# Loading the last nine rounds' input in mid-run, in three loads of three rounds, in a kernel that writes all pairwise products

## Chip, cores, metric

One core of a Trainium2 chip. The metric is device time in microseconds (us), the median of several executions. Every run told of here was at a granted clock of 1.0.

## The reference

```python
# inputs: (4096, 256) float32
d = inputs.shape[1]
dot = jnp.einsum('bi,bj->bij', inputs, inputs)
iu, ju = jnp.triu_indices(d)
return dot[:, iu, ju]          # (4096, 32896) float32
```

4.2 MB come in and 539 MB go out; there is one multiplication per output.

## The kernel before

The input is a tile `xt` of 128 partitions with 32 rows each. A round is two rows per partition, so there are 16 rounds. The output columns of a round are cut into five chunks; VectorE (DVE) and ScalarE (ACT) share the products of a chunk, and two stores send it out. Three output buffers rotate. The very first chunk is stored in four pieces, so that the stores begin early.

```python
opool = ctx.enter_context(tc.tile_pool(name="o", bufs=3))
...
cuts = [0, REPEAT * d, total // 2, total]        # rounds 0, 1-7, 8-15
for a, b in zip(cuts, cuts[1:]):
    nc.sync.dma_start(xt[:, a:b], x_in[:, a:b])

for g in range(groups):                          # 16 rounds
    for c, (lo, hi) in enumerate(zip(borders, borders[1:])):   # 5 chunks
        o = opool.tile([P, REPEAT, slot], F32, tag="o", ...)
        first = g == c == 0
        cuts = [lo, *(FIRST if first else []), hi]
        for a, b in zip(cuts, cuts[1:]):
            ...                                  # products on ACT and DVE
            for r in range(REPEAT):
                nc.sync.dma_start(x_out[g][:, r, a:b], o[:, r, a - lo : b - lo])
```

Loads and stores all go through SyncE's queue.

Of the kernel before, what the change touches and what calls it, by code (L numbers as in the profile page):

```python
# [1 line left out]

# [4 lines left out]

F32 = mybir.dt.float32
AF = mybir.ActivationFunctionType
ALU = mybir.AluOpType  # L10

P = 128
UNIT = 64
REPEAT = 2
PIECES = 5
BUDGET = 0.95
FIRST = [512, 1536, 3584]


def even_borders(lo: int, hi: int, pieces: int) -> list[int]:  # L20
    units = (hi - lo) // UNIT
    return [lo + units * c // pieces * UNIT for c in range(pieces)] + [hi]


def runs(d: int, lo: int, hi: int) -> list:


    found, at = [], 0
    for i in range(d):
        a, b = max(at, lo), min(at + d - i, hi)  # L30
        if a < b:
            found.append((i, i + a - at, a, b - a))
        at += d - i
    return found


def vector_ops(block: list) -> list:




    ops, k = [], 0
    while k < len(block):
        i, j, at, n = block[k]
        m = 2 if k + 2 < len(block) and i == j else 1
        ops.append((block[k], m))
        k += m
    return ops


def interleave(block: list) -> list:


    half = len(block)
    while half and len(vector_ops(block[:half])) > len(vector_ops(block[half:])):
        half -= 1
    a, b = vector_ops(block[:half]), vector_ops(block[half:])
    return [op for k in range(max(len(a), len(b))) for ops in (a, b) for op in ops[k : k + 1]]


def vector_time(block: list) -> float:
    return sum(68 + 1.046 * REPEAT * n * m for (*_, n), m in vector_ops(block))


def split(block: list, budget: float) -> int:


    scalar, k = 0.0, 0
    while k < len(block):
        scalar += REPEAT * (184 + 0.837 * block[k][3])  # L70
        if vector_time(block[k:]) <= budget or scalar > vector_time(block[k + 1 :]):
            break
        k += 1
    return k


def window(ap: bass.AP, free: list) -> bass.AP:
    return bass.AP(ap.tensor, ap.offset, [list(ap.ap[0]), *free])


@with_exitstack
def kernel(
    ctx: ExitStack, tc: tile.TileContext, x: bass.AP, out: bass.AP
):





    nc = tc.nc  # L90
    n, d = x.shape
    width = out.shape[1]
    assert n % (P * REPEAT) == 0 and width == d * (d + 1) // 2 and width % UNIT == 0
    groups = n // (P * REPEAT)
    borders = even_borders(0, width, PIECES)
    slot = max(b - a for a, b in zip(borders, borders[1:]))

    xpool = ctx.enter_context(tc.tile_pool(name="x", bufs=1))
    opool = ctx.enter_context(tc.tile_pool(name="o", bufs=3))

    x_in = x.rearrange("(p r) d -> p (r d)", p=P)
    x_out = out.rearrange("(p g r) c -> g p r c", p=P, r=REPEAT)


    total = n // P * d
    xt = xpool.tile([P, total + 1], F32, name="x")
    nc.vector.memset(xt[:, total:], 0.0)  # L107
    cuts = [0, REPEAT * d, total // 2, total]
    for a, b in zip(cuts, cuts[1:]):
        nc.sync.dma_start(xt[:, a:b], x_in[:, a:b])  # L110

    for g in range(groups):
        for c, (lo, hi) in enumerate(zip(borders, borders[1:])):
            o = opool.tile([P, REPEAT, slot], F32, tag="o", name=f"o_{g}_{c}")
# [3 lines that stand above are left out]
                block = runs(d, a, b)  # L118
                k = split(block, 0.0 if first else BUDGET * REPEAT * (b - a))
                for i, j, at, length in block[:k]:  # L120
                    for r in range(REPEAT):
                        row = (g * REPEAT + r) * d
                        nc.scalar.activation(  # L123
                            o[:, r, at - lo : at - lo + length],
                            xt[:, row + j : row + j + length],
                            AF.Copy,
                            scale=xt[:, row + i : row + i + 1],
                        )
                row = g * REPEAT * d
                for (i, j, at, length), m in interleave(block[k:]):  # L130
                    at -= lo
                    nc.vector.tensor_tensor(  # L132
                        o[:, :, at : at + m * length],
                        window(xt[:, row + j :], [[d, REPEAT], [1, m], [1, length]]),
                        window(xt[:, row + i :], [[d, REPEAT], [1, m], [0, length]]),
                        ALU.mult,
                    )
                for r in range(REPEAT):
                    nc.sync.dma_start(x_out[g][:, r, a:b], o[:, r, a - lo : b - lo])  # L139


# [1 line left out]
_INS = ["r_inputs"]  # L143
_OUTS = [((4096, 32896), "float32")]


# [20 lines left out]
```

## Time and profile before

| | before |
|---|---|
| time, median (range) of 3 runs | 1274.32 us (1274.27 to 1274.36) |
| bytes through the store and load queue | 543.17 MB |
| share of the span in which the transfer engines work for it | 99.8% |
| VectorE / ScalarE busy | 78% / 38% |

The kernel is a queue with compute in front of it. One therefore looks first at when the queue is idle or slow, and at compute only where the queue waits for it. The prediction below shows the lines. One view it doesn't show is needed later: the stretches of the kernel before around the time when chunk 1 is issued (26.69 us). In the stretches the columns are start and end, length, busy time of the engines with the number of instructions, clock, share of the transfer engines, GB/s.

### The profile page before, as it was taken

The numbers are of one execution on the slowest core, as the hardware profiler recorded it, in microseconds if no ns is written. First come the engines' busy times: TensorE is split into PE (matmuls) and PEld (weight loads), VectorE is DVE, ScalarE is ACT, GpSimd is POOL, SyncE is SP. The second block draws the span as 40 slices with busy tenths as digits, with TensorE's granted clock in tenths as the row PEclk, the third lists the DMA queues.
The fourth block names the chain that finished last, engine by engine and source line by source line (L and its number), as shares of the span: only waits on it lengthen the run. The fifth ranks groups of instructions, "written<-read, shape, count | busy, mean of one in ns | idle before, by whom it ended". The sixth has DMA issues, their size and how long they took to land.

```text
span 1272.5 us, 3975 instructions
## 1 busy us (share of the span) xinstructions
DVE 996.1 (78%) x1813; ACT 486.7 (38%) x1547; POOL 0.2 (0%) x4
## 2 busy tenths in 40 slices
DVE  8987887878777787777877777777777777777770
ACT  5523535234342433424334252342523425234250
POOL 0000000000000000000000000000000000000000
DMA  9999999999999999999999999999999999999998
GB/s 384 435 433 430 434 433 427 434 432 427 431 428 432 429 430 431 429 431 429 433 427 431 429 431 429 431 430 430 429 432 427 433 427 432 428 432 429 431 427 346
DMA packets 24367, 543.43 MB, mean 427 GB/s; under 512 B 2704, under 2 KB 2704, under 8 KB 3344
## 3 DMA queue, kind: packets, MB, share of 16 engines
q1 hardware_dynamic: 24336, 543.17, 99.8%
q14 instruction: 31, 0.25, 0.0%
HBM read 4.19 MB, written 538.97 MB: 427 GB/s over the span
## 4 chain that ended last, share of the span: by engine, by line
DMA 70%; DVE 25%; issue 1%; SPq 1%; DVEq 0%
DMA out_dram<-o 70%; DVE o L132 25%; SPq L139 1%; DMA x<-in_r_inputs_dram 1%; DVEq L132 0%; SPq L110 0%
## 5 line engine op out<-in xcount | busy, mean ns | idle before, releaser
L132 DVE TENSOR_TENSOR o<-x 128x356 f32<-128x356 f32 (+61 forms) x1812 | 996.1, 634 | 239.9 <-DMA out_dram<-o 191.1
L123 ACT ACTIVATE o<-x 128x253 f32<-128x253 f32 (+41 forms) x1546 | 485.4, 404 | 748.6 <-DMA out_dram<-o 732.8
L123 ACT ACT_TABLE_LOAD x1 | 1.3, 1283 | 0.7 <-PEq L154 0.7
L107 DVE MEMSET x<- 128x1 f32 x1 | 0.1, 59 | 0.8 <-PEq L154 0.8
L154 POOL MEMSET const-uint8-127<- 128x1 uint8 x1 | 0.1, 102 | 0.0
L154 POOL MEMSET const-bfloat16-1.0<- 128x1 bf16 x1 | 0.1, 101 | 0.0
L154 POOL MEMSET const-float32-0.0<- 128x1 f32 x1 | 0.1, 98 | 0.2 <-issue 0.2
L154 POOL MEMSET const-float32-1.0<- 128x1 f32 x1 | 0.1, 98 | 0.0
## 6 DMA issues: line engine op xcount, KB each, us to landing
out_dram<-o SPq DMA_DIRECT2D x128, 3296.0 KB, 27.2
out_dram<-o SPq DMA_DIRECT2D x30, 3264.0 KB, 28.9
out_dram<-o SPq DMA_DIRECT2D x2, 1472.0 KB, 13.3
x<-in_r_inputs_dram SPq DMA_DIRECT2D x1, 2048.0 KB, 12.3
out_dram<-o SPq DMA_DIRECT2D x2, 1024.0 KB, 10.0
x<-in_r_inputs_dram SPq DMA_DIRECT2D x1, 1792.0 KB, 6.8
out_dram<-o SPq DMA_DIRECT2D x2, 512.0 KB, 10.2
out_dram<-o SPq DMA_DIRECT2D x2, 256.0 KB, 10.0
```

The costliest lines, as they stand in the source:

```text
L107: nc.vector.memset(xt[:, total:], 0.0)
L123: nc.scalar.activation(o[:, r, at - lo : at - lo + length], xt[:, row + j : row + j + length], AF.Copy, scale=xt[:, row + i : row + i + 1],)
L132: nc.vector.tensor_tensor(o[:, :, at : at + m * length], window(xt[:, row + j :], [[d, REPEAT], [1, m], [1, length]]), window(xt[:, row + ...
L139: nc.sync.dma_start(x_out[g][:, r, a:b], o[:, r, a - lo : b - lo])
L154: nc = _bacc.Bacc("TRN2", target_bir_lowering=False, num_devices=1)
```

## The change

Its intent: only the input of the first seven rounds is fetched before the stores begin; the rest follows in mid-run, so that the first stores don't wait behind input that is not needed for hundreds of microseconds.

```diff
+AHEAD = 7
+LOADED = 3
...
-    cuts = [0, REPEAT * d, total // 2, total]
-    for a, b in zip(cuts, cuts[1:]):
+    def load(g: int, end: int):
+        a, b = g * REPEAT * d, end * REPEAT * d
         nc.sync.dma_start(xt[:, a:b], x_in[:, a:b])
+    load(0, 1)
+    load(1, AHEAD)
...
                 for r in range(REPEAT):
                     nc.sync.dma_start(x_out[g][:, r, a:b], o[:, r, a - lo : b - lo])
+            if c == 0 and g and g % LOADED == 0 and g - LOADED + AHEAD < groups:
+                load(g - LOADED + AHEAD, min(g + AHEAD, groups))
```

## The prediction

> **What bounds the kernel now.** I read the page's summary first, for busy shares, slices and queues.
>
> ```profile
> span 1272.5 us, 3975 instructions
> DVE 996.1 (78%) x1813; ACT 486.7 (38%) x1547; POOL 0.2 (0%) x4
> ...
> DMA  9999999999999999999999999999999999999998
> GB/s 384 435 433 430 434 433 427 434 432 427 431 428 432 429 430 431 429 431 429 433 427 431 429 431 429 431 430 430 429 432 427 433 427 432 428 432 429 431 427 346
> ...
> q1 hardware_dynamic: 24336, 543.17, 99.8%
> ...
> HBM read 4.19 MB, written 538.97 MB: 427 GB/s over the span
> ```
>
> The one queue keeps 16 transfer engines busy for 99.8% of the span; VectorE (DVE) is busy for 78% and ScalarE (ACT) for 38%. The kernel is bound by bytes: 543.17 MB at about 430 GB/s. The change moves no byte away, so in mid-run there is nothing to gain. Only the first slice (384 GB/s) and the last (346) fall short. The end is the same in both kernels, so the question is the start. The waits show the steady state: both engines wait for buffers that a store has to free, that is, for the queue.
>
> ```profile
> ACT o L123 <- DMA out_dram<-o: 732.8, 75, 12.5
> DVE o L132 <- DMA out_dram<-o: 191.1, 59, 4.0
> ```
>
> Next the timeline of the first 60 us (start, length) and, of the transfer issues of the loads, the time to landing.
>
> ```profile
> 0.73 1.34 SPq L110 DMA_DIRECT2D x<-in_r_inputs_dram  x3
> ...
> 3.41 4.28 DVE L132 TENSOR_TENSOR o<-x 128x512 f32<-128x512 f32 x9 [2.55 <-DMA x<-in_r_inputs_dram]
> ...
> 8.02 52.23 DVE L132 TENSOR_TENSOR o<-x 128x988 f32<-128x988 f32 x90 [0.33 <-DMA x<-in_r_inputs_dram]
> ```
>
> ```profile
> x<-in_r_inputs_dram SPq DMA_DIRECT2D x1, 2048.0 KB, 12.3
> ...
> x<-in_r_inputs_dram SPq DMA_DIRECT2D x1, 1792.0 KB, 6.8
> ```
>
> Two things to see. VectorE starts at 3.41, when only the first load (round 0) is in; the second lands near 8 us and the third near 13 us. And from 8.02 on it runs without a gap. So the ramp up is set by compute, unless the queue is behind it. Which of the two it is, the stretches with the transfer share and GB/s (last two columns) and the store issues tell.
>
> ```profile
> 1.50:2.00 0.50, 0.00 (x0) 0.50 (x1) 0.00 (x0) 1.00 0.35 49
> 2.00:7.00 5.00, 3.59 (x8) 3.60 (x11) 0.00 (x0) 1.00 1.04 406
> ...
> 0.00:26.69 26.69, 23.01 (x33) 17.07 (x45) 0.20 (x4) 1.00 0.94 374
> ...
> 30.00:1260.00 1230.00, 969.79 (x1777) 469.63 (x1502) 0.00 (x0) 1.00 1.00 430
> ```
>
> ```profile
> 26.69 0.84 SPq L139 DMA_DIRECT2D out_dram<-o  x2
> ```
>
> I call a fifth of the output columns of one round (two rows per partition) a chunk; the first chunk is stored in four pieces of 512, 1024, 2048 and 2944 columns. Their stores are issued at 4.80, 6.74, 11.21 and 14.40 us (same timeline, in short windows); those of chunk 1 at 26.69 us. By then the queue has moved 26.69 us x 374 GB/s = 9.98 MB, out of the loads (4.19 MB) and chunk 0 (128 partitions x 2 rows x 6528 columns x 4 B = 6.68 MB), together 10.87 MB. So it is 0.89 MB, or 2.1 us, behind when chunk 1 arrives, and gets to it at about 28.8 us. That 2.1 us is all that fewer bytes at the start can win.
>
> **What the Trainium skill says.** "DMA: Bandwidth & Descriptors", section Queues, rings and completion order: descriptors on one ring are consumed in ring order. The trace agrees: the first store, issued at 4.80, takes some 10 us to land behind the loads. So a load in mid-run takes its turn in the same line as the stores and displaces them by its own length. The same page, section Where 436 GB/s comes from, puts the ceiling of the fabric at 435 GB/s; the steady 430 here is within 1.2% of it, which leaves no idle room in which a load could hide. The same page, section Latency and other measured facts, gives a memory access as 0.2 us on average and 2 us at high load; the trace of before has no load beside stores in mid-run, so it doesn't show this, and I keep it as a risk.
>
> **The change part by part.**
> Removed from the start: the first loads now bring rounds 0 to 6 and not 0 to 15. That is 9 rounds x 512 floats x 4 B x 128 partitions = 2.36 MB less, 5.5 us at 430 GB/s. The remaining 1.84 MB are in when the queue has moved as much, at about 6.5 us (49 GB/s for 0.5 us, then 406).
>
> What the queue does with the time: piece 1 (0.52 MB, issued 4.80) goes from 6.5 to 7.8; piece 2 (1.05 MB, issued 6.74) to 10.3. Piece 3 is issued at about 11 us, since VectorE makes it by then. From an issue to the first bytes are some 1.2 us here (first load: issued 0.73, bytes just before 2.0). So it runs from 12.2 to 17.1, and piece 4 (3.0 MB, issued 14.40) to 24.1. Then the queue is empty until chunk 1. VectorE saves its wait of 0.33 us at 8.02 (the load that it waits for is 0.26 MB, 0.6 us, shorter), so chunk 1 is issued at 26.4 and its bytes start at 27.6. Before they start at 28.8. **Gain at the start: 1.2 us**, and not 5.5: the rest turns into idle time of the queue, near 11 and from 24 to 27.6 us.
>
> After that the queue doesn't run dry again: a chunk takes 6592 x 1024 B = 6.75 MB, 15.7 us, to store and about 12.4 us to compute; chunk 2 was issued at 39.0, while chunk 1 goes on until 43.3.
>
> Added in mid-run: three loads of 0.786 MB, each 1.83 us of the full queue. All of it is on the path that sets the end, since the queue is always backed up. **Cost: 5.5 us.**
>
> Added inefficiency: loads are not quite at full rate. In before the second load moved some 2 MB at 406, an excess of 0.3 us; the third had 2.1 MB from 7 to 13 us, 6.0 us in place of 4.9, an excess of about 1 us. I take 0.3 us for each of the smaller new loads, towards the low end. **Cost: 0.9 us.**
>
> Issues and waits: three issues of 0.42 us on SyncE, hidden behind a backlog of more than a store. The buffers come free 1.8 us later after each load, but the product of the delay is again the queue's time, already counted. Nothing is computed anew.
>
> Sum: 1274.3 - 1.2 + 5.5 + 0.9 = **1279.5 us**, 0.4% slower.
>
> **The rivals.**
> (a) Dependence by whole tile: the mid-run load writes the tile of the input that every operation reads. If the order is kept for the whole tile, the operations after each load wait until it lands. A store takes 27.2 us from issue to landing in steady state; the load behind it would land 2 us later, with an empty queue, which then waits some 12.4 us of compute and 2 to 3 us of latencies. Three times 15 is 45 us: about 1320 us. Against it: in before VectorE started at 3.41 while two loads into the same tile were under way; only the operation at 8.02 waited, one of those on a pair of rows, whose window reaches one element into the next round. So the order is kept by region, and of rounds 0 to 6 only round 6 reaches into round 7's region, long after its load. I give this 3%.
> (b) The queue never empties at the start, or loads and stores overlap, so that the mid-run loads cost nothing: time 1273 us, at best. For it: the third load's slow stretch (1 us) leaves the start. Against it: chunk 1's issue time is VectorE's, which runs without a gap, and in the trace loads occupy the engines at no higher rate than stores do. I give 8%.
> (c) Loads among stores are slow, a packet taking twice as long while the memory is loaded with writes: each costs another 1.8 us, or 1284 to 1286 us. For it: the slow third load. Against: that slow stretch had no stores beside it at all, so the cause is another. I give 12%.
>
> **Range and chances.** The middle case, 77%, spans the excess of the loads from 0 to 1 us each and the uncertainty of 1 us at the start: 1277.5 to 1281.5. I widen it towards (c) and somewhat towards (b): 1276.5 to 1283.0. Two per cent are 25 us: only (a) reaches that. Faster by over 2% would need 25 us less transfer, and the bytes are the same: 0.5%. Slower by over 2%: 3.5%. Within 2%: 96%.
>
> **What would show it right or wrong.** In the profile after: the first slice's rate falls from 384 to about 325 GB/s (1.84 + 6.68 MB, and 1.8 MB of chunk 1 from 27.6 on, over 31.8 us); the first two loads land 0.6 us earlier; VectorE's wait of 0.33 us at 8 us is gone; chunk 1 is issued at 26.4; the transfer share of the whole falls to some 99.4%; the slices with a mid-run load still show 430 GB/s, with 0.79 MB of it being input; the waits of VectorE for the input stay under 4 us. The prediction is wrong if VectorE waits for a load in mid-run (a), if the slices with loads show clearly more than 435 GB/s (b), or if they fall by more than some 10 GB/s each (c). It is also wrong if chunk 1's issue comes earlier than 26 us.

## More of the kernel before

```profile
24.00:25.00 1.00, 1.00 (x2) 0.00 (x0) 0.00 (x0) 1.00 0.99 424
25.00:26.00 1.00, 1.00 (x2) 0.00 (x0) 0.00 (x0) 1.00 1.03 436
26.00:27.00 1.00, 1.00 (x3) 0.00 (x0) 0.00 (x0) 1.00 0.99 424
```

The queue is full: it still works on chunk 0.

## The result, and the profile after

| | before | after |
|---|---|---|
| time, median | 1274.30 us (4 runs, one more than above) | 1279.12 us (1278.81 to 1279.59, 4 runs) |
| span of the profiled run | 1272.5 us | 1277.3 us |
| ratio | | 1.0038 (95%: 1.0021 to 1.0055) |

A ratio is the mean time of one kernel's runs over that of the other's in the same rounds, so not quite the ratio of the medians. It is 4.8 us slower by the medians, and also by the two profiled spans.

The page of the kernel after, the lines that answer to those of before:

```profile
span 1277.3 us, 3976 instructions
...
GB/s 358 435 429 428 435 423 434 431 426 435 427 431 432 425 435 410 430 434 431 432 433 431 422 424 432 432 434 433 431 430 432 430 427 435 424 434 430 427 434 322
...
q1 hardware_dynamic: 24624, 543.17, 99.5%
```

The first slice fell from 384 to 358. In mid-run one slice stands out with 410, the 16th (479 to 511 us), and a pair of 422 and 424 (the 23rd and 24th). A page like this dates the loads. There are two such places, and not three. The prediction had named a fall of more than some 10 GB/s in such a slice as a sign of rival (c), slow loads among stores; the 410 is such a fall.

The timeline of SyncE, first 60 us of the kernel after, tells where the third one is:

```profile
4.79 2.77 SPq L145 DMA_DIRECT2D out_dram<-o  x4
7.60 0.79 SPq L113 DMA_DIRECT2D x<-in_r_inputs_dram  x1
10.78 41.73 SPq L145 DMA_DIRECT2D out_dram<-o  x10
```

A load at 7.60 us: the program's scheduler moved the first of the three forward, from round 3 to the space between the stores of the second and the third piece, where SyncE had nothing to do. The built program's order shows it too (a listing of SyncE's instructions, not a profile):

```
L145 DMACopy out_dram<-o_0_65 128x1024 [waits Activation_49]
L113 DMACopy x<-in_r_inputs_dram 128x1536
L145 DMACopy out_dram<-o_0_65 128x2048 [waits DVE_49,Activation_49]
```

It waits for nothing, since no operation had read its target. The diff alone doesn't show this. The two other loads were issued where the source puts them:

```profile
467.39 1.25 SPq L113 DMA_DIRECT2D x<-in_r_inputs_dram  x1
...
705.95 1.26 SPq L113 DMA_DIRECT2D x<-in_r_inputs_dram  x1
```

The stretches of the kernel after, at the start:

```profile
11.00:12.00 1.00, 1.00 (x2) 1.00 (x4) 0.00 (x0) 1.00 0.47 156
12.00:13.00 1.00, 1.00 (x2) 1.00 (x4) 0.00 (x0) 1.00 0.85 285
...
25.00:26.00 1.00, 1.00 (x3) 0.00 (x0) 0.00 (x0) 1.00 0.56 236
26.00:27.00 1.00, 1.00 (x3) 0.00 (x0) 0.00 (x0) 1.00 0.06 24
27.00:28.00 1.00, 1.00 (x3) 0.56 (x2) 0.00 (x0) 1.00 1.00 422
```

and the issue of chunk 1's stores, from the timeline of SyncE:

```profile
26.25 0.81 SPq L145 DMA_DIRECT2D out_dram<-o  x2
```

The early load lies where the queue would have been short of work (11 to 13 us), and the queue still runs dry before chunk 1, which VectorE has ready at 26.25 us. Chunk 1's bytes flow from about 27.1 us; in before the queue came to them at about 28.8. The packet records agree: chunk 1's first packet starts at 27.08 us, and in before at 28.81. (The packed trace holds start, length and size of every packet; no view of the profile prints them one by one.) So the start gained 1.7 us. The span grew by 4.8 us, so from there on 6.5 us were lost, for two loads whose bytes alone take 2 x 1.83 = 3.7. What the rest is, the stretches around the second load show (it was issued at 467 us and is carried out when the stores ahead of it are):

```profile
492.00:494.00 2.00, 2.00 (x3) 0.00 (x0) 0.00 (x0) 1.00 0.97 418
...
496.00:497.00 1.00, 0.73 (x3) 0.00 (x0) 0.00 (x0) 1.00 1.71 418
497.00:498.00 1.00, 0.00 (x0) 0.00 (x0) 0.00 (x0) 1.00 0.29 89
498.00:499.00 1.00, 0.00 (x0) 0.00 (x0) 0.00 (x0) 1.00 1.03 253
499.00:500.00 1.00, 0.00 (x0) 0.00 (x0) 0.00 (x0) 1.00 0.89 303
500.00:501.00 1.00, 0.00 (x0) 0.00 (x0) 0.00 (x0) 1.00 1.26 525
```

These are not all equally exact: a packet seems to be booked whole to one stretch, so a 1 us stretch can read over 1 or over the steady rate. The sum is safer: 418, 89, 253, 303 and 525 are 1588 over 5 us, 318 GB/s on average, where the steady rate is 430. That is 5 x (1 - 318/430) = 1.3 us lost around this one load. Its packet records put part of that on the load's own packets and part on the last stores before it, which took 1.6 to 2.0 us instead of 0.98.

No operation waited for a load in mid-run. The waits of the kernel after:

```profile
DVE o L138 <- DMA out_dram<-o: 205.5, 62, 5.7
...
DVE o L138 <- DMA x<-in_r_inputs_dram: 2.5, 1, 2.5
```

The one wait for the input is that at the very start; the 0.33 us at 8 us are gone.

### The profile page after: what moved, and what is told of

Its sections match the earlier page's. It is cut to its first block, busy times and chain, and to the rows that moved or that the text cites. A ratio compares the mean times of both kernels' runs of the same rounds, so it can differ in the third digit from the quotient of the medians.

```text
span 1277.3 us, 3976 instructions
## 1 busy us (share of the span) xinstructions
DVE 995.6 (78%) x1813; ACT 486.6 (38%) x1547; POOL 0.2 (0%) x4
## 3 DMA queue, kind: packets, MB, share of 16 engines
q1 hardware_dynamic: 24624, 543.17, 99.5%
## 4 chain that ended last, share of the span: by engine, by line
DMA 70%; DVE 25%; SPq 1%; issue 1%; DVEq 0%
DMA out_dram<-o 70%; DVE o L138 25%; SPq L145 1%; DMA x<-in_r_inputs_dram 0%; DVEq L138 0%
```

## The experiments

My theory after the result: a load in mid-run costs its bytes and 1.4 us on top, for the change of direction in the queue; the early load was nearly free because it lay in an idle gap. The 1.4 is (6.5 - 3.7) / 2. The rivals: the excess goes with the bytes; any small transfer among large ones pays it; or it is not the loads in mid-run at all.

Each time stands beside about 1274.2 to 1274.3 us for the kernel before on the same chip.

### One: let all three loads be in mid-run (the first attempt missed)

Rounds 7 to 9 go to the places of rounds 0 to 2, so that their load can't be issued before round 2 is used up. (Here and in number nine the cut leaves out a renamed variable, the same index in the lines that compute, and one or two memsets of one column, which moved the first store from 4.79 to 4.95 and 5.01 us.)

```diff
+    def slot(g): return g - AHEAD if AHEAD <= g < AHEAD + LOADED else g
...
-        nc.sync.dma_start(xt[:, a:b], x_in[:, a:b])
+        at = slot(g) * REPEAT * d
+        nc.sync.dma_start(xt[:, at : at + b - a], x_in[:, a:b])
```

> All three loads truly in mid-run: rounds 7 to 9 take the places of rounds 0 to 2, so the first of the three can't be issued at 7.6 us any more. Theory (a mid-run load costs its bytes, 1.83 us, and about 1.4 us for the change of direction in the queue; the first load of the changed kernel lay in an idle gap of the start): about 1282.4 us, 3.2 over the changed kernel, with chunk 1 starting at the same 27.1 us. Rival (my prediction's arithmetic, 1.83 + 0.3 us a load): 1281.2. Rival (the early first load cost as much as one in mid-run, the gap hid nothing): 1279.1, as the changed kernel.

Measured: 1279.32 us (ratio 1.0040), as the changed kernel. But its timeline has an early load again:

```profile
7.76 1.03 SPq L119 DMA_DIRECT2D x<-in_r_inputs_dram  x1
```

In the built program this is the load of rounds 10 to 12, which the scheduler now moved forward; it had nothing to wait for either. So the kernel was not what I meant it to be, and it says nothing between the theory and its rival. The mended one comes as number nine.

### Two: no load in mid-run

```diff
+                if first and b == FIRST[1]:
+                    load(AHEAD, groups)          # rounds 7-15 after piece 2
...
-            if c == 0 and g and g % LOADED == 0 and ...:
-                load(...)
```

> No load in mid-run: after the second piece of chunk 0 one load brings rounds 7 to 15. Theory: the queue gets through its 10.87 MB by about 28.8 us as in the kernel before, and nothing follows in mid-run: 1273.5 to 1275. Rival (the change's cost is something else than loads in mid-run, for example the split of the loads at the start): near 1279.

Measured: 1275.04 us, ratio 1.0007 (0.9992 to 1.0022). The interval includes no difference, but all four times (from 1274.83) lie above all seven of the kernel before (up to 1274.37), so it is rather 0.8 us slower. Splitting and delaying the loads within the start costs at most that; the greater part of the 4.8 us comes from the loads after it.

### Three and four: the same bytes in eight or in one load of mid-run

```diff
-LOADED = 3
+LOADED = 1          # three
```
```diff
-            if c == 0 and g and g % LOADED == 0 and ...:
-                load(...)
+            if c == 0 and g == 3:  load(AHEAD, 10)      # four
+            if c == 0 and g == 6:  load(10, groups)
```

> The nine rounds in nine loads of one round, the first again in the start, eight in mid-run. Theory (1.4 us per change of direction, whatever the size): 1274.3 - 1.7 + 8 x (0.61 + 1.4) = 1288.7. Rival (the excess goes with the bytes, 1.4 us per 0.79 MB): 1281.2. Rival (prediction's arithmetic, no excess by direction): about 1278.

> As the changed kernel, but the second and third load are one, of six rounds, at round 6. Theory (cost per change of direction): one less, 1277.7. Rival (excess with the bytes): 1279.1, as the changed kernel.

Measured: 1280.80 us with eight small loads (256 KB) in mid-run, 1277.60 us with one of 1536 KB. The second is as the theory said: one change of direction less, 1.5 us less than the changed kernel. The first is not: it should have been 1288.7, and it is nearer to the excess by bytes (1281.2). Neither "1.4 us whatever the size" nor "by the bytes" fits both. With the 1.7 us of the start taken off, they give an excess of 0.4 us for each load of 256 KB, and of 1.4 us for the one of 1536 KB.

### Five to eight: the cost of one added transfer, by itself

The start is left as before, and transfers that nobody needs are added in mid-run, after the first chunk of a round: 12 loads of 768 KB, 12 of 256 KB, 12 stores of 768 KB, 6 loads of 2304 KB. The difference to before, divided by their number, is the price of one.

```diff
+            if c == 0 and g >= 4:                        # five; six: g - 1; eight: g >= 10, rounds 0-8
+                a, b = (g - 3) * REPEAT * d, g * REPEAT * d
+                nc.sync.dma_start(xt[:, a:b], x_in[:, a:b])
```
```diff
+            if c == 0 and 3 <= g < groups - 1:           # seven: a place overwritten by the last round
+                nc.sync.dma_start(x_out[groups - 1][:, 0, : 3 * REPEAT * d], xt[:, : 3 * REPEAT * d])
```

> The kernel before, with its start untouched, and 12 added loads in mid-run that bring again the three rounds just used (768 KB each, nobody reads them). Theory (1.83 us of bytes and 1.4 us per change of direction): 12 x 3.2 = 39, 1313 us. Rival (bytes alone): 12 x 1.83 = 22, 1296.3. Prediction's arithmetic (2.13 each): 1299.9.

> The same with 12 loads of one round (256 KB, 0.61 us each). Theory (1.4 us each on top, whatever the size): 1298.4. Rival (the excess goes with the bytes): 12 x 1.08 = 13, 1287.2. Bytes alone: 1281.6.

> The kernel before and 12 added stores of the same 768 KB, in the same 6 KB runs, to a place of the output that is overwritten at the end; no added load. Theory (the excess comes from the change of direction): bytes alone, 12 x 1.83 = 22, 1296.3. Rival (the excess comes from any small transfer between the large ones): 1313, as with loads.

> The kernel before and 6 added loads of nine rounds (2304 KB, 5.49 us each) in mid-run. Theory (1.4 us each on top): 6 x 6.9 = 41, 1315.6. Rival (the excess goes with the bytes, 4.2 us each): 1332.

| added | time, us | per transfer | its bytes (at number seven's rate) | excess |
|---|---|---|---|---|
| five: 12 loads of 768 KB | 1313.79 | 3.29 | 1.85 | 1.44 |
| six: 12 loads of 256 KB | 1285.93 | 0.97 | 0.62 | 0.35 |
| seven: 12 stores of 768 KB | 1296.55 | 1.85 | 1.85 | (0) |
| eight: 6 loads of 2304 KB | 1309.49 | 5.87 | 5.56 | 0.30 |

Number seven settles one thing: a store of the same bytes, in the same runs of 6 KB, after the first chunk of a round too (one round earlier), costs its bytes and nothing more. The excess belongs to loads among stores. And a load of the change's size has an excess of 1.44 us, as the theory took from the changed kernel. But the excess neither is constant nor grows with the size: 0.35, 1.44 and 0.30. (The 0.38 in an expectation below is the last one, with the bytes counted at 430 GB/s. The four times of number eight spread over 2.3 us, 0.4 us for each of its loads.)

### Nine: all three loads truly in mid-run

As number one, but every later load takes used places (7 to 15 go to 0 to 8), and in the built program each stands where the source puts it (the first was issued at 231.75 us).

```diff
-        return g - AHEAD if AHEAD <= g < AHEAD + LOADED else g
+        return g - AHEAD if g >= AHEAD else g
```

> The first experiment mended: there the scheduler had issued another of the three loads early. Now every one of them takes the place of rounds that are used up, and in the built program each stands behind the first chunk of rounds 3, 6 and 9. Theory (the early load of the changed kernel lay in idle time; a 768 KB load in mid-run costs 3.3 us by the runs with 12 added loads): 1279.2 + 3.3 = 1282.5. Rival (the early load was as dear as one in mid-run): 1279.2. Prediction's arithmetic, 2.1 per load: 1281.3.

Measured: 1282.64 us (1282.55 to 1282.97). One more load in mid-run costs 3.5 us more than in the changed kernel, where that load lay in the start. In the gap it was nearly free. The stretches of this kernel show the gap empty:

```profile
10.00:12.00 2.00, 2.00 (x5) 2.00 (x7) 0.00 (x0) 1.00 0.46 184
...
24.00:25.00 1.00, 1.00 (x2) 0.32 (x1) 0.00 (x0) 1.00 0.01 0
```

In the first line the queue works for less than half of the time, waiting for piece 3; in the second, and until 27 us, it has nothing to do at all. Chunk 1 begins no earlier for it, since VectorE sets its time.

### Ten and eleven: the place or the size of the load?

Loads of 768 KB had moved through the input, those of 2304 KB were always of the same place. These runs swap that.

```diff
-                a, b = (g - 3) * REPEAT * d, g * REPEAT * d
+                a, b = 0, 3 * REPEAT * d                 # ten, on five
```
```diff
-                nc.sync.dma_start(xt[:, : 9 * REPEAT * d], x_in[:, : 9 * REPEAT * d])
+                a, b = (g - 9) * REPEAT * d, g * REPEAT * d   # eleven, on eight
+                nc.sync.dma_start(xt[:, a:b], x_in[:, a:b])
```

> The 12 added loads of 768 KB again, but each brings rounds 0 to 2, always the same place. The excess over the bytes was 1.44 us per 768 KB load with moving places and 0.38 us per 2304 KB load with a fixed one. If the place of the source (or its being read again) makes the difference: 12 x (1.83 + 0.4) = 27, 1301. If the size of the pieces does: 1313.8, as with the moving ones.

> The 6 added loads of 2304 KB again, but of the nine rounds last used, so that the place moves by 2 KB per partition each time. If the place makes the difference: 6 x (5.49 + 1.44) = 41.6, 1316. If the size does: 1309.5, as with the fixed place.

Measured: 1314.27 and 1310.39 us, as five and eight. The place in the input makes no difference. What is left is the size of the loads, though the two pairs differ also in the number of loads (12 and 6) and in when they come (rounds 4 to 15 and 10 to 15). The number is hardly it: with 768 KB two, three and twelve loads (the changed kernel, number nine, number five) cost 1.4 to 1.5 us each over their bytes. The time in the run was not varied alone. Why the size should matter so, with 1.4 us at 1536 KB in number four and 0.3 to 0.5 at 2304 KB, stays open.

### Twelve: the added loads from another queue

```diff
-                nc.sync.dma_start(xt[:, a:b], x_in[:, a:b])
+                nc.scalar.dma_start(xt[:, a:b], x_in[:, a:b])
```

> The 12 added loads of 768 KB (moving places), issued from ScalarE's queue, so that they don't stand in line behind the stores. If the bytes and the mixing of directions cost, wherever the load stands: 1310 to 1318 us, as from the one queue (1313.8). If the excess comes from the change of direction inside one ring: nearer 1296 (bytes alone).

Measured: 1296.79 us (1296.62 to 1297.69), 1.88 us per load. That is the price of the bytes (1.85), and 17 us less than the same 12 loads in the stores' queue (number ten, in the same session on the same chip, took 1314.27). The page of this kernel shows the loads as a queue of their own, q10:

```profile
q1 hardware_dynamic: 24336, 543.17, 98.0%
q10 hardware_dynamic: 1728, 9.44, 1.7%
```

Where the excess is in number five, and is not in number twelve, the end of the run shows best, since all 16 transfer engines must be done. Number five:

```profile
1288.00:1292.00 4.00, 0.00 (x0) 0.00 (x0) 0.00 (x0) 1.00 0.99 428
1292.00:1296.00 4.00, 0.00 (x0) 0.00 (x0) 0.00 (x0) 1.00 0.49 211
1296.00:1300.00 4.00, 0.00 (x0) 0.00 (x0) 0.00 (x0) 1.00 0.40 171
1300.00:1304.00 4.00, 0.00 (x0) 0.00 (x0) 0.00 (x0) 1.00 0.26 112
1304.00:1308.00 4.00, 0.00 (x0) 0.00 (x0) 0.00 (x0) 1.00 0.14 59
```

and number twelve:

```profile
1284.00:1288.00 4.00, 0.00 (x0) 0.00 (x0) 0.00 (x0) 1.00 0.86 369
1288.00:1292.00 4.00, 0.00 (x0) 0.00 (x0) 0.00 (x0) 1.00 0.20 88
1292.00:1295.90 3.90, 0.00 (x0) 0.00 (x0) 0.00 (x0) 1.00 0.07 27
```

A share of 0.49 means that over the stretch about half of the engines still work. In number five they come in one after the other over some 17 us; in number twelve all but three or so are done together, and the last follow within 7. So in number five some engines were delayed more than others, and the slowest sets the time. That the delays add up, the packet records show: from the first engine that is done to the last it is 5.7 us in before, 7.5 with two such loads (the changed kernel), 9.0 with three (number nine) and 17.4 with twelve (number five). That is not the whole excess: in number five even the first engine is done 5 us later than the bytes explain, and number four, with 1.4 us of excess, has a spread of only 5.6. How the hardware does this is not shown: number twelve changes the queue, and with it also how loads and stores are interleaved and when they run.

None of these versions beats the kernel before.

## Why the prediction was right

The time (1279.12 us against 1279.5, range 1276.5 to 1283.0) came out; the chain behind did only in part, and the close hit is partly luck.

- **The bound.** Right. The share of the queue went from 99.8 to 99.5% (I had said 99.4), and no engine's waits changed their nature. Rival (a), order by whole tile, is out: VectorE waited for input 2.5 us in all. Rival (b) is out: number two moves all bytes in the start and doesn't win, and added loads never cost less than their bytes.
- **The gain at the start: 1.2 us.** Right in kind and near in size: 1.7. Chunk 1 was issued at 26.25 (I had said 26.4), and its first bytes flowed some 0.8 us after the issue and not 1.2. Of the 5.5 us, 1.7 were won, 1.8 went to the load that the scheduler put back into the start, and the rest, about 2.0 by this sum, turned into idle time of the queue.
- **Three loads in mid-run, 5.5 us.** Wrong as a step. Only two were in mid-run, 3.7 us; the scheduler had put the first into the idle time that the change itself had opened. My first slice (325 GB/s, measured 358) missed for the same reason; in number nine it is 332.
- **0.3 us of inefficiency per load.** Wrong in size: 1.4, by the changed kernel and by number five. I had taken it from two loads that stood in front of the stores; among stores, in their queue, it is another thing. My sign that slices with loads stay at 430 GB/s failed with it (410). I had put such an excess into rival (c) with 1.8 us, but with the wrong cause: a memory busy with stores. In number twelve the memory is as busy (427 GB/s over the span, 422 in number five) and the excess is 0.03. Which cause is right stays open.

The two wrong steps cancel, and that is luck: 5.5 + 0.9 predicted, 3.7 + 2.8 measured, with 1.2 and 1.7 off for the start. The kernel that I had in mind is number nine, and for it my sum of 1279.5 was 3.1 us too low: by the measured terms it is 1274.3 - 1.7 + 5.5 + 3 x 1.4 = 1282.3, and it took 1282.64.

## What to carry to other kernels

In a kernel bound by one queue, ask before moving a transfer later whether the queue has work for the time that this frees; here chunk 1's bytes could begin only 1.7 us sooner, and the rest became idle or was filled by the early load. If loads must go among stores, try another queue: the 12 added loads cost 0.03 us over their bytes from there, and 1.44 in the stores' queue (this was tried with 768 KB alone, and not with the change itself). Or keep them in the start. And read from the built program, or from the timeline, where a transfer was really issued, before counting it: the scheduler may have moved it, as it did here with one of three, and in my first experiment with another.

## What the Trainium skill lacked or had wrong

- "DMA: Bandwidth & Descriptors", section Issuing engines are not separate DMA queues, says that issuing from several engines at once will only save the sequencer's time to initiate a transfer. Here the kernel with 12 added loads of 768 KB took 1313.79 us with them in the stores' queue and 1296.79 with them in ScalarE's. The difference of 17 us is no issue time, as the store queue had work waiting: a store of number five landed 30.8 us (median) after its issue.
- No page that I read gives the price of a load among stores in one queue: here 1.4 us beyond the bytes for 768 KB, and for one of 1536 KB, and 0.3 to 0.5 for 256 and 2304 KB; for a store in its place, nothing.
- The first page again, section Why a DMA increments its semaphore by 16 and not by 1, says that the engines of a transfer finish independently, but not that such delays add up over a run: half of the engines were done some 17 us before the last one in number five. Even in the kernel before about three engines work on alone at the end:

```profile
1266.00:1268.00 2.00, 0.00 (x0) 0.00 (x0) 0.00 (x0) 1.00 0.18 79
```
